# Collected words in four loads on ScalarE's queue, their tables on SyncE's, cleared by VectorE, and a third buffer for the turned adjacency

## The chip, the cores and the metric

The kernel runs on one core of a Trainium2 chip. A time is the device time of one execution in microseconds, the median of several executions. A profiled execution gives a trace besides, from which the stretches and waits below are read. The engines are called PE (TensorE), PEld (its weight loads), DVE (VectorE), ACT (ScalarE), POOL (GpSimd) and SP (SyncE). SP and ACT issue nearly all DMA transfers here, each in its own program order.

## What is computed

A stack of four graph layers on 16 graphs of 1024 nodes with 64 channels, each layer added to its input after a layer norm and a relu. Nearly all of what is difficult lies in the first layer, which drops some edges and then takes, for every node and channel, a weighted sum of three quantiles over the node's neighbours:

```python
rem = neigh & (sk > 1) & (rank % sk == sk - 1) & mask[:, :, None]
rem = rem | jnp.swapaxes(rem, 1, 2)
nd = jnp.where(rem, 0.0, adj_) > 0
s = jnp.sort(jnp.where(nd[..., None], x[:, None, :, :], jnp.inf), axis=2)
nv = nd.sum(2)
for tau, w in zip((0.25, 0.5, 0.75), (0.25, 0.5, 0.25)):
    pos = tau * (nv - 1)
    lo, hi = floor(pos), ceil(pos)
    agg = agg + w * (s[lo] + (pos - lo) * (s[hi] - s[lo]))
y = relu((x + agg) @ W1 + b1) @ W2 + b2
```

The second layer is a gated unit over relu(A m), the third a small network over x and A h, the fourth a graph attention with a softmax over 0.8 A + 0.2 e. All three use the whole adjacency A, so each graph's 4 MB adjacency is needed both as it is and turned.

## The kernel before

The 16 graphs are handled in eight pairs. For every pair there are five kinds of work.

- `sort_pair` and `sort_begin` sort each channel's values over the nodes (DVE, with loads and stores through DRAM on SP's queue).
- `neighbours` reads the adjacency row block by row block (`a`, L819, SP), makes the neighbour bits (L820 DVE, L821 POOL) and their running count (L825 DVE), and turns each 128 x 512 piece on PE (L831). ACT copies the turned piece from PSUM into a tile `at` (L832, two buffers, L833) and stores it to DRAM as `a_d` (L834, ACT's queue). A further stage on ACT and DVE marks the dropped edges, and PE writes their transposes (L875).
- `weights` and `select` find the quantiles. The kept-edge matrix times one-hot codes of the sorted values gives packed counts, "words", by matmul (L1040); ACT and DVE compare them (L1050, L1098, L1114), and PE picks the values by a table `vtab` (L1143), filled by 24 small loads on SP's queue (L930). A node whose words do not suffice is collected: `compact`, at the end of `select`, computes the missing words of up to 64 collected nodes of a batch (L1231), ACT copies them to `xr` (L1237), and SP stores them to DRAM as `x_d` in four pieces (the pieces are those of `PIECES`, two groups of 512 columns each, the last of one).
- `extras` does for the collected nodes of both batches what `select` did for the others: it loads their words (`comb_x`, L1250, one transfer of 1792 KB on SP's queue), clears two tables `tab0`, `tab1` (L1254, POOL) and fills each by four small loads (L1256, ACT's queue), computes `qx` (L1262, DVE), and for three quantiles compares the words (`y_x` L1268 ACT, transposes L1275 PE, `sign_x` L1278 ACT, maxima DVE). PE picks the values (`cand`, L1299, from `tab` and `sign_x`), DVE sums them (L1006, L1013, L1015), PE spreads the sums to their nodes with `sel_t` (L1307, L1310), and a predicated copy writes them into the aggregate.
- `layers` runs the four layers, loading the turned adjacency `adjT` from `a_d` (SP).

The pairs overlap by hand-written program order: `layers` of a pair is written first, then `neighbours` and `sort_pair` of the next pair and `sort_begin` of the one after it. The Tile framework's scheduler merges these into one fixed order per engine when the kernel is compiled; at run time each engine goes through its list in order and waits on semaphores where an operand or a buffer isn't ready. An engine's DMA issues stand in the same list as its other instructions. The work of later pairs thus fills `extras` and `layers`, and starts already at the end of `select`. The last pair has nothing to be filled with, and the first is preceded by about 437 us in which the first sort and the first `neighbours` run alone.

Tiles of `extras` are in a pool `xs`, those of `neighbours` in a pool `nb` that is open beside `xs` and `layers`.

Of the kernel before, what the change touches and what calls it, by code (L numbers as in the profile page):

```python
# [9 lines left out]
F32 = mybir.dt.float32  # L10
# [13 lines left out]
P = 128  # L24
# [18 lines left out]
def gnn_stack(ctx, tc, x, adj, nodemask, w, out):  # L43
# [10 lines left out]
    nc = tc.nc  # L54
# [101 lines left out]
    x_d = dram.tile([P, NW * C], F32, name="x_d")  # L156
# [648 lines left out]
    def neighbours(b, ndT, row10, qb, qz, nb, nbp):  # L805
# [9 lines left out]
        for t0 in range(0, NT, HT):  # L815
            cum = nb.tile([P, HT, N], F16, name="cum")
            for t in range(t0, t0 + HT):
                a = nb.tile([P, N], F32, name="a", bufs=2)
                nc.sync.dma_start(a, adj[b, t * P : (t + 1) * P, :])  # L819
                nc.vector.tensor_single_scalar(ni[:, t, :], a, 0.0, op=ALU.is_gt, saturate=False)  # L820
                nc.gpsimd.tensor_mul(  # L821
                    ni[:, t, t * P : (t + 1) * P], ni[:, t, t * P : (t + 1) * P], offdiag, saturate=False
                )

                nc.vector.tensor_tensor_scan(  # L825
                    cum[:, t - t0, :], ni[:, t, :], wide[:, t, pad - 1 : pad - 1 + N], 0.0, op0=ALU.add, op1=ALU.add
                )
                for q in range(0, NT, 4):
                    pt = nbp.tile([P, 4, P], F32, name="pk")
                    for k in range(4):  # L830
                        nc.tensor.transpose(pt[:, k, :], a[:, (q + k) * P : (q + k + 1) * P], ident)  # L831
                    at = nb.tile([P, 4, P], F32, name="at", bufs=2)  # L832
                    nc.scalar.copy(at, pt)  # L833
                    nc.scalar.dma_start(  # L834
                        a_d[b % 4, q : q + 4, :, t * P : (t + 1) * P].rearrange("j p n -> p j n"), at
                    )


            sk = nb.tile([P, 4, HT], F32, name="sk")
            nc.vector.tensor_tensor(sk[:, 2, :], cum[:, :, N - 1], ni[:, t0 : t0 + HT, N - 1], op=ALU.add)  # L840
            nbi = nb.tile([P, HT], I32, name="nbi")
            nc.vector.tensor_scalar_add(nbi, sk[:, 2, :], 2.0)
            nc.vector.tensor_single_scalar(nbi, nbi, 2, op=ALU.logical_shift_right)
            nc.vector.tensor_single_scalar(sk[:, 0, :], sk[:, 2, :], 2 * MAX_DEGREE, op=ALU.is_gt)
            nc.vector.tensor_mul(sk[:, 0, :], sk[:, 0, :], mask[:, t0 : t0 + HT])
            nc.vector.tensor_copy(sk[:, 1, :], nbi)
            nc.vector.scalar_tensor_tensor(sk[:, 1, :], sk[:, 1, :], 1.0, sk[:, 0, :], op0=ALU.add, op1=ALU.mult)
            nc.vector.tensor_scalar(sk[:, 2, :], sk[:, 1, :], -3.0, 4.0, op0=ALU.mult, op1=ALU.add)
            nc.vector.tensor_scalar_add(sk[:, 1, :], sk[:, 1, :], -1.0)
            nc.vector.scalar_tensor_tensor(sk[:, 3, :], sk[:, 1, :], -1.0, sk[:, 1, :], op0=ALU.mult, op1=ALU.mult)  # L850
            for t in range(t0, t0 + HT):
                k = t - t0
                sq = nb.tile([P, N], F32, name="sq")
                nc.scalar.activation(sq, cum[:, k, :], AF.Square, bias=sk[:, 2, k : k + 1], scale=1.0)  # L854
                nc.scalar.activation(sq, sq, AF.Square, bias=sk[:, 3, k : k + 1], scale=1.0)
                nc.scalar.activation(rem[:, t, :], sq, AF.Relu, bias=one, scale=-1.0, saturate=False)  # L856


                for blocks, to in (
                    ([(j, t) for j in range(t + 1)], ndT[:, : t + 1, t * P : (t + 1) * P]),  # L860
                    ([(t, i) for i in range(t)], ndT[:, t, : t * P].rearrange("p (i n) -> p i n", n=P)),
                ):
                    for n, (j, i) in enumerate(blocks):
                        if n % 4 == 0:
                            pk = nbp.tile([P, 4, P], F32, name="pk")
                        terms = [
                            (ni[:, i, j * P : (j + 1) * P], ident_b),
                            (rem[:, i, j * P : (j + 1) * P], minus_b),
                            (minus_b, rem[:, j, i * P : (i + 1) * P]),
                        ]  # L870
                        if i == j:
                            terms.append((ident_b, ident_b))
                        last = n % 4 == 3 or n == len(blocks) - 1
                        for m, (lhs, rhs) in enumerate(terms):
                            nc.tensor.matmul(  # L875
                                pk[:, n % 4, :], lhs, rhs, start=(n % 4 == 0 and m == 0),
                                stop=(m == len(terms) - 1 and last),
                            )
                        if last:
                            n0, m = n - n % 4, n % 4 + 1  # L880
                            nc.scalar.activation(to[:, n0 : n + 1, :], pk[:, :m, :], AF.Relu, saturate=False)
# [22 lines left out]
        nc.vector.tensor_sub(coef[:, :, :, 0], shares, coef[:, :, :, 1])  # L904


    def weights(b, sb):

        node = sb.tile([P, NT, 4, C], F16, name="node")
        nc.sync.dma_start(node[:, :, 0, :], y_d[b])
        positive = sb.tile([P, NT, C], BF16, name="positive", bufs=2)
        nc.sync.dma_start(positive, p_d[b])
        for k in range(1, 4):
            nc.vector.tensor_scalar_add(node[:, :, k, :], node[:, :, 0, :], 4.0 * CODE * k)
        wt = {}
        for g in PIECES:
            wt[g] = sb.tile([P, NT, 8, C], F8, name="wt", bufs=len(PIECES) + 2)
            for k in range(0, 8, 4):  # L920
                nc.vector.tensor_scalar(  # L921
                    wt[g][:, :, k : k + 4, :].bitcast(U8), node, 4.0 * (25 + CODE * (8 * g + k)), 4.0 * 26,
                    op0=ALU.add, op1=ALU.min,
                )
        rows = w_d[b * C : (b + 1) * C]
        for part, d_, w0, n in ((0, 4, 0, 32), (1, 4, 40, 32), (2, 16, 32, 8)):
            src = rows.rearrange("(q d) w e -> d w q e", d=d_)
            to = vtab[:, part].rearrange("p (q d e) -> p q d e", d=d_, e=24)
            for d in range(d_):
                nc.sync.dma_start(to[d : d_ * n : d_, :, d, :], src[d, w0 : w0 + n])  # L930
        return wt, positive


# [312 lines left out]
    def extras(pr, kept, aggs, xs, xp):  # L1246

        vx = kept["vx"]
        comb = xs.tile([P, NW * C], F32, name="comb_x")
        nc.sync.dma_start(comb, x_d)  # L1250
        tabs = []
        for i in range(2):
            tab = xs.tile([4 * NH, NQ, 4, 48], F16, name=f"tab{i}")
            nc.gpsimd.memset(tab, 0.0)  # L1254
            for d in range(4):
                nc.scalar.dma_start(  # L1256
                    tab[d : 4 * NH : 4, :, d, :],
                    t_d[(pr * 2 + i) * C : (pr * 2 + i + 1) * C, :NH].rearrange("(q d) h e -> d h q e", d=4)[d],
                )
            tabs.append(tab)  # L1260
# [44 lines left out]
        for i in range(2):  # L1305
            sel_t = xs.tile([P, NT, P], F32, name="sel_t")
            nc.sync.dma_start(sel_t, sel_d[i])  # L1307
            ps = xp.tile([P, 2, 512], F32, name="tr")[:, 0, :].rearrange("p (t c) -> p t c", c=C)
            for t in range(NT):
                nc.tensor.matmul(ps[:, t, :], sel_t[:, t, :], aggx, start=True, stop=True)  # L1310
            nc.vector.copy_predicated(
                aggs[i], kept["flag"][i].rearrange("p (t o) -> p t o", o=1).to_broadcast([P, NT, C]), ps
            )


    def layers(b, side_, agg, ly, lb):
# [235 lines left out]
    with nb_ as nb, nbp_ as nbp:  # L1552
        sort_pair(0, sort_begin(0, nbp), nbp)
        made = prepare(0, nb, nbp)
        if pairs > 1:
            cur = sort_begin(1, nbp)
    for pr in range(pairs):
        with tc.tile_pool(reuse_waits="tile", name="keep", bufs=1) as keep:
            aggs = [keep.tile([P, NT, C], F32, name=f"agg{i}") for i in range(2)]
# [4 lines left out]
            with tc.tile_pool(reuse_waits="tile", name="kn", bufs=1) as kn:  # L1564
                with (
# [4 lines left out]
                    tc.tile_pool(reuse_waits="tile", name="sc", bufs=2, space=PSUM) as sc,  # L1570
                ):
                    for i in range(2):
                        wt, positive = weights(pr * 2 + i, kn)
                        select(pr * 2 + i, i, wt, positive, *made[i], aggs[i], kept, sw, sg, sy, sc, sp)
            nb_, nbp_ = side_pools()
            with nb_ as nb, nbp_ as nbp:
                with tc.tile_pool(reuse_waits="tile", name="xs", bufs=1) as xs, tc.tile_pool(reuse_waits="tile", name="xp", bufs=1, space=PSUM) as xp:
                    extras(pr, kept, aggs, xs, xp)
                with (
                    tc.tile_pool(reuse_waits="tile", name="ly0", bufs=1) as ly0,  # L1580
                    tc.tile_pool(reuse_waits="tile", name="ly1", bufs=1) as ly1,
# [57 lines left out]
```

## Time and profile before

| quantity | value |
| --- | --- |
| median of 3 runs | 6583.64 us (6575.58 to 6585.77) |
| the profiled execution | 6593.77 us |
| its span, first to last instruction | 6592.0 us |
| mean granted TensorE clock | 0.821 |
| one pair, from y_x to the next pair's y_x, first seven pairs | 771 to 781 us |
| DMA engines' mean rate | 86 GB/s |

A pair's stretch between the last copy of collected words (L1237) and the first `y_x` (L1268) is called its front below. The first `y_x` of the eight pairs starts at 926.6, 1700.6, 2481.1, 3252.2, 4029.7, 4806.2, 5580.0 and 6315.0 us. From there to the end of `extras` are 94 to 100 us in the first seven pairs and 78 us in the last, and then 189 to 195 us of `layers` in every pair.

How to read the lines that follow: a group line gives line, engine, operation, out<-in with the size, and count; then busy us, mean ns of one; then the idle time of its engine just before it and what ended most of that. The chain is followed back from the last instruction, at each step to what released it.

### The profile page before, as it was taken

How to read it: one execution, taken by the hardware profiler on the slowest of the kernel's cores; microseconds unless marked ns; L12 is line 12 of the kernel's file. 1: busy time of each engine (PE TensorE's matmuls, PEld its weight loads, DVE VectorE, ACT ScalarE, POOL GpSimd, SP SyncE). 2: the span in 40 equal slices, each digit the busy share in tenths (PEclk: the TensorE clock that was granted, in tenths of full speed). 3: DMA queues.
4: the chain of work that ended last, by engine and by line, in shares of the span. 5: the costliest groups of instructions: out<-in, count | busy, mean ns of one | idle time of the engine just before them, and what ended most of it. 6: DMA issues, size and time to landing. Idle time of an engine off the chain costs nothing.

```text
span 6592.0 us, 112930 instructions
## 1 busy us (share of the span) xinstructions
PE 4547.7 (69%) x45010; PEld 2830.8 (43%) x45010; DVE 5323.9 (81%) x13015; ACT 3548.0 (54%) x4348; POOL 180.7 (3%) x250
## 2 busy tenths in 40 slices
PE   0167858777577776778587785777757876778856
PEld 0144544355434444355443554344543544435532
DVE  7759985999769996799949997599967999576645
ACT  0165646556456556565555565556555664555623
POOL 0000000000000000000000000000010000000000
PEclk9868868888688887889788886888868887788967
DMA  1320136211451124401262114511145013520024
GB/s 56 111 70 32 58 99 186 65 44 46 131 177 40 49 87 143 128 33 58 84 189 75 38 52 118 181 52 50 61 146 150 32 56 91 168 76 16 7 61 133
DMA packets 522184, 568.15 MB, mean 86 GB/s; under 512 B 264620, under 2 KB 414510, under 8 KB 520622
## 3 DMA queue, kind: packets, MB, share of 16 engines
q1 hardware_dynamic: 353056, 488.35, 24.3%
q10 hardware_dynamic: 167822, 70.38, 3.8%
q8 instruction: 355, 5.82, 0.4%
q0 software_dynamic: 768, 2.10, 0.1%
q14 instruction: 183, 1.50, 0.1%
HBM read 376.95 MB, written 183.76 MB: 85 GB/s over the span
## 4 chain that ended last, share of the span: by engine, by line
PE 45%; DVE 22%; ACT 17%; DMA 12%; issue 4%; ACTq 0%; SPq 0%; POOL 0%; DVEq 0%; POOLq 0%
PE comb L1040 18%; PE cand L1143 6%; ACT sign L1098 6%; PE comb L1096 5%; PE bank L1401 4%; DMA adjT<-a_d 4%; DMA a_d<-at 3%; ACT y L1050 2%; PE comb L1231 2%; DVE y L1114 2%; DVE cum L825 2%; DVE att L1511 2%; PE pk L875 1%; DVE adjT L1505 1%; DMA a<-in_adj_dram 1%
## 5 line engine op out<-in xcount | busy, mean ns | idle before, releaser
L1040 PE MATMUL comb<-wt,ndT 128*128 128x512 fp8e5 x6144 | 1496.2, 400 | 26.1 <-DVE wt L921 9.0
L1050 ACT ACTIVATE y<-comb,qb 128x1024 int16<-128x1024 f32 (+1 forms) x640 | 630.6, 1026 | 957.0 <-PE comb L1040 956.5
L1040 PEld LDWEIGHTS <-ndT 128*128 128x128 fp8e5 x6144 | 612.9, 103 | 763.2 <-issue 155.3
L1114 DVE TENSOR_TENSOR y<-y 128x512 uint16<-128x512 uint16 (+5 forms) x896 | 702.9, 789 | 65.7 <-PE comb L1096 51.7
L1143 PE MATMUL cand<-vtab,sign 128*128 128x48 f16 (+1 forms) x18432 | 685.2, 193 | 63.4 <-ACT sign L1098 29.2
L1143 PEld LDWEIGHTS <-sign 128*128 128x128 fp8e5 x18432 | 653.8, 97 | 135.0 <-issue 34.6
L1096 PE MATMUL comb<-ident_b,y 128*128 128x128 bf16 x4608 | 390.6, 254 | 434.2 <-ACT sign L1098 381.4
L1098 ACT ACTIVATE sign<-comb,half 128x2048 fp8e5<-128x2048 int16 (+1 forms) x384 | 591.6, 1541 | 127.2 <-PE comb L1096 118.4
L1098 ACT ACTIVATE sign<-comb,lower 128x2048 fp8e5<-128x2048 int16 (+1 forms) x384 | 591.0, 1539 | 0.0
L1151 DVE COPY_PREDICATED cand<-w_f,cand 128x256 f32<-128x256 uint16 (+1 forms) x1536 | 528.3, 376 | 68.4 <-PE cand L1143 66.3
L1096 PEld LDWEIGHTS <-y 128*128 128x128 bf16 x4608 | 356.9, 115 | 458.1 <-issue 451.6
L825 DVE TENSOR_TENSOR_SCAN cum<-ni 128x1024 f16<-128x1024 fp8e5 x128 | 292.8, 2294 | 124.1 <-ACT sq L854 107.0
L1401 PE MATMUL bank<-adjT,nd 128*64 128x512 f32 x1024 | 322.1, 685 | 77.8 <-DMA adjT<-a_d 73.1
L1401 PE MATMUL bank<-att,hs 128*64 128x512 f32 x512 | 210.1, 905 | 197.7 <-ACT hs L1516 197.2
L875 PE MATMUL pk<-ident_b,ni 128*128 128x128 bf16 x1024 | 221.8, 242 | 152.9 <-ACT at L833 87.6
L833 ACT COPY at<-pk 128x512 f32<-128x512 f32 x256 | 146.9, 585 | 319.6 <-DMA a_d<-at 241.5
L729 DVE TENSOR_TENSOR swapped<-s 128x512 uint16<-128x512 f32 x440 | 302.0, 686 | 8.8 <-ACT s L717 2.7
L736 DVE TENSOR_TENSOR s<-s 128x512 f32<-128x512 f32 (+2 forms) x440 | 288.3, 655 | 0.0
L737 DVE TENSOR_TENSOR s<-s 128x512 f32<-128x512 f32 (+2 forms) x440 | 288.2, 655 | 0.0
L921 DVE TENSOR_SCALAR wt<-node 128x2048 uint8<-128x2048 f16 x224 | 265.6, 1219 | 21.8 <-PE comb L1231 21.7
L875 PE MATMUL pk<-minus_b,rem 128*128 128x128 bf16 x1024 | 225.8, 247 | 77.8 <-ACT rem L856 77.8
L760 DVE TENSOR_TENSOR code<-code,xo 128x1024 uint16<-128x1024 uint16 x360 | 265.7, 738 | 5.1
(300 smaller groups left out, 8132.6 us busy)
## 6 DMA issues: line engine op xcount, KB each, us to landing
adjT<-a_d SPq DMA_DIRECT2D x384, 512.0 KB
a<-in_adj_dram SPq DMA_DIRECT2D x128, 512.0 KB
a_d<-at ACTq DMA_DIRECT2D x256, 256.0 KB
m_d<-swapped SPq DMA_DIRECT2D x104, 512.0 KB
swapped<-m_d SPq DMA_DIRECT2D x104, 512.0 KB
n_d<-nat SPq DMA_DIRECT2D x128, 128.0 KB
comb_x<-x_d SPq DMA_DIRECT2D x8, 1792.0 KB
x_d<-xr SPq DMA_DIRECT2D x48, 256.0 KB
```

Source lines behind the costliest of these rows:

```text
L729: nc.vector.tensor_tensor(side(swapped[:, k, :], j), hi, lo, op=ALU.is_gt)
L736: nc.vector.tensor_tensor(to_lo, lo, hi, op=ALU.max)
L825: nc.vector.tensor_tensor_scan(cum[:, t - t0, :], ni[:, t, :], wide[:, t, pad - 1 : pad - 1 + N], 0.0, op0=ALU.add, op1=ALU.add)
L875: nc.tensor.matmul(pk[:, n % 4, :], lhs, rhs, start=(n % 4 == 0 and m == 0), stop=(m == len(terms) - 1 and last),)
L1040: nc.tensor.matmul(pw[:, e, :], ndT[:, j, t * P : (t + 1) * P], piece[:, j].rearrange("p w c -> p (w c)"), start=(j == 0), stop=(j == NT - 1),
L1050: nc.scalar.activation(y[:, 0, chunks, at : at + words_ * d_].rearrange("p q (w d) -> p q w d", d=d_), by_word[:, : words_ * C].rearrange( ...
L1096: nc.tensor.transpose(pt[:, q - q0, :], y[:, 0, q, :].bitcast(BF16), ident_b)
L1098: nc.scalar.activation(signs[tl][s][:, q0:q1, :], pt.bitcast(I16), AF.Sign, bias=before[s], scale=-1.0, saturate=False,)
L1114: nc.vector.tensor_tensor(v[:, :, :, :n], v[:, :, :, :n], v[:, :, :, n : 2 * n], op=ALU.max)
L1143: nc.tensor.matmul(cand[:, e, at : at + 12 * d_].rearrange("p (d l) -> p d l", l=12), signs[tl][sec][:, chunk, :], tab[:, q, :, half_ * 12 ...
L1151: nc.vector.copy_predicated(v[:, :, :, dst : dst + k], mk.to_broadcast([P, 2, C // 2, k]), v[:, :, :, frm : frm + k])
L1401: nc.tensor.matmul(po[to : to + C, :], lhs, rhs[:, f * HALF : (f + 1) * HALF], start=(j == 0), stop=(j == NT - 1))
```

## The change

Five edits. The `comb_x` load becomes four loads by the pieces of `x_d` (three of 512 KB, one of 256 KB), issued on ACT's queue instead of SP's. The tables are cleared by DVE instead of POOL. Their eight loads a pair are issued on SP's queue instead of ACT's. `extras` returns the last of these loads, and `weights` of the next pair's first batch tells the scheduler to put the first of its `vtab` loads, and those after it, behind that load in SP's order of issue. The turned adjacency `at` has three buffers instead of two, 2 KB more in each partition.

```diff
@@ neighbours
-                    at = nb.tile([P, 4, P], F32, name="at", bufs=2)
+                    at = nb.tile([P, 4, P], F32, name="at", bufs=3)
@@ weights
-    def weights(b, sb):
+    def weights(b, sb, behind):
...
+        order = ExitStack()
         rows = w_d[b * C : (b + 1) * C]
         for part, d_, w0, n in ((0, 4, 0, 32), (1, 4, 40, 32), (2, 16, 32, 8)):
             src = rows.rearrange("(q d) w e -> d w q e", d=d_)
             to = vtab[:, part].rearrange("p (q d e) -> p q d e", d=d_, e=24)
             for d in range(d_):
+                if behind is not None:
+                    order.enter_context(tc.issue_after(behind))
+                    behind = None
                 nc.sync.dma_start(to[d : d_ * n : d_, :, d, :], src[d, w0 : w0 + n])
+        order.close()
         return wt, positive
@@ extras
         comb = xs.tile([P, NW * C], F32, name="comb_x")
-        nc.sync.dma_start(comb, x_d)
+        for u in range(0, len(PIECES), 2):
+            at = slice(PIECES[u] * 512, (PIECES[u] + len(PIECES[u : u + 2])) * 512)
+            nc.scalar.dma_start(comb[:, at], x_d[:, at])
         tabs = []
         for i in range(2):
             tab = xs.tile([4 * NH, NQ, 4, 48], F16, name=f"tab{i}")
-            nc.gpsimd.memset(tab, 0.0)
+            nc.vector.memset(tab, 0.0)
             for d in range(4):
-                nc.scalar.dma_start(
+                taken = nc.sync.dma_start(
                     tab[d : 4 * NH : 4, :, d, :],
                     t_d[(pr * 2 + i) * C : (pr * 2 + i + 1) * C, :NH].rearrange("(q d) h e -> d h q e", d=4)[d],
                 )
...
+        return taken.ins if hasattr(taken, "ins") else taken
@@ the loop over pairs
+    taken = None
     for pr in range(pairs):
...
-                        wt, positive = weights(pr * 2 + i, kn)
+                        wt, positive = weights(pr * 2 + i, kn, None if i else taken)
...
-                    extras(pr, kept, aggs, xs, xp)
+                    taken = extras(pr, kept, aggs, xs, xp)
```

## The prediction

> **What bounds the kernel now.** I read the page first (parts 1 and 4), then the stretch in which the edited lines stand. The page names no single engine as the bound:
>
> ```profile
> PE 4547.7 (69%) x45010; PEld 2830.8 (43%) x45010; DVE 5323.9 (81%) x13015; ACT 3548.0 (54%) x4348; POOL 180.7 (3%) x250
> PE 45%; DVE 22%; ACT 17%; DMA 12%; issue 4%; ACTq 0%; SPq 0%; POOL 0%; DVEq 0%; POOLq 0%
> L833 ACT COPY at<-pk 128x512 f32<-128x512 f32 x256 | 146.9, 585 | 319.6 <-DMA a_d<-at 241.5
> ```
>
> DVE is busiest, yet only 22% of the chain that ended last is DVE: latencies in turn set the time, so a stall can be worth its full length where nothing fills it. The copy of the turned adjacency (L833) costs 146.9 us and stands 241.5 us more waiting until an earlier store has freed one of its two buffers.
>
> Second, the tile that the change moves off ACT and POOL:
>
> ```profile
> L1256 ACTq DMA_DIRECT2D tab<-t_d x64: 782/785/5817, 918.8 to 6314.1; - x64
> L1254 POOL MEMSET tab<- x16: 2657/2657/2802, 904.8 to 6290.3; 112x3072 f16 x16
>   ACT y_x L1268: 74.5, 5
> ```
>
> Third, ACT's timeline at the start of extras of the third pair, typical of the middle ones (columns: start, us, what, idle before it and what ended that):
>
> ```profile
> 2447.72 0.58 ACT L1237 COPY xr<-comb 64x512 f32<-64x512 f32 x1 [1.65 <-DMA x_d<-xr]
> 2463.00 0.59 ACT L833 COPY at<-pk 128x512 f32<-128x512 f32 x1 [2.16 <-DMA a_d<-at]
> 2466.23 0.59 ACT L833 COPY at<-pk 128x512 f32<-128x512 f32 x1 [2.65 <-DMA a_d<-at]
> 2467.31 13.70 ACTq L1256 DMA_DIRECT2D tab<-t_d  x8
> 2481.06 6.46 ACT L1268 ACTIVATE y_x<-comb_x,qx 128x3584 int16<-128x3584 f32 x2 [14.24 <-DMA vtab<-w_d]
> ```
>
> The last collected words are copied at 2448.3, and the first use of them (y_x) begins at 2481.06: 33 us in which ACT does eight L833 copies with their waits (to 2466.9) and then stands in eight table issues. SP's timeline has the load of comb_x issued at 2463.56, and its queue events land it at 2474.47, 10.9 us later: y_x could have begun 6.6 us sooner. The chain of this stretch shows why the eight issues took 13.7 us and not 8 x 0.785 = 6.3: the first waited for POOL's two clears, later ones for other loads, down to a vtab load of SP's.
>
> ```profile
> 2462.74 4.57 POOL tab L1254 x2
> 2467.31 10.57 DMA tab<-t_d
> 2477.90 0.59 SPq L930
> 2478.53 2.54 DMA vtab<-w_d
> ```
>
> Fourth, the windows table (columns: busy us of PE, PEld, DVE, ACT, POOL, then clock, DMA share, GB/s) for this front, the rest of extras and the layers, and the last pair's front:
>
> ```profile
> 2448.00:2481.00 33.00, 10.08 (x172) 8.53 (x170) 31.95 (x73) 4.89 (x9) 8.81 (x9) 0.75 0.87 251
> 2481.00:2579.00 98.00, 58.34 (x799) 49.40 (x799) 68.64 (x149) 66.10 (x71) 3.06 (x7) 0.65 0.33 95
> 2579.00:2768.00 189.00, 139.62 (x722) 63.69 (x723) 129.63 (x350) 106.31 (x153) 7.69 (x10) 0.83 0.57 171
> 6302.00:6315.00 13.00, 4.89 (x144) 4.67 (x144) 7.08 (x27) 0.03 (x1) 0.00 (x0) 0.85 0.77 235
> ```
>
> In the front DVE is full, but with fill (neighbours and sorting of later pairs); the DMA engines are 0.87 busy. The front is 31.6 to 33.4 us long in the first seven pairs and 13 in the last, which has no next pair beside it.
>
> **What the Trainium skill says.** "DMA: Bandwidth & Descriptors", section "Issuing engines are not separate DMA queues": transfers started by different engines run on the same 16 DMA engines, and spreading them saves only the issuing sequencer's time. The trace agrees: ACT loses 0.785 us for each table issue while its loads share an 0.87 busy front. So moving the comb_x load to ACT makes it no faster; only issuing it sooner could. Same page, "Anatomy of one DMA — SWDGE (gpsimd) path": DMA engines wait on no semaphore, the issuing sequencer does. The trace agrees for these queues: y_x stood behind issues that waited. "VectorE: DVE Perf Modes", section "Zero memsets can be issued as uint32 (trn2)": a clear costs a cycle an element, and a 2-byte one can go at half the elements. The trace has this for vtab (L142: 2304 uint32 in 1.978 us, 0.859 ns each), so a table of 3072 f16, 1536 words, is 1.32 us.
>
> **Part by part.** Sums are against the profiled execution, 6593.77 us (span 6592.0); the median of the runs, 6583.64, is 10.1 lower, and I take savings from that.
>
> *Tables off ACT's queue.* ACT loses eight issues a pair. y_x then waits for comb_x alone. On ACT the four pieces of that load follow the eight L833 copies, because the program order that the compiler keeps puts extras' first instructions beside the end of the values (DVE's qx at 2466.39, right behind the last sum), not where x_d has landed (2452.6 by the queue's events). With three buffers the eight copies end some 4 us earlier: first piece at about 2462.5, four issues of 0.8, landing 10.9 us after the first as the single load did, since bytes and traffic are the same: 2473.4. y_x gains 2481.0 - 2473.4 = 7.6 us. Seven pairs: 53. In the last pair, comb_x is issued at 6304.64 and lands at 6313.29, with y_x at 6314.97; the two DVE clears now precede qx (6311.2 + 2.6 = 6313.8): gain 1.2. From both sides: nothing, if pieces land later on the busy engines, and 20 us a pair, if they go out once x_d is there (2452.6 + 8.65 = 2461.3, the landing of a quiet load).
>
> *Clears on DVE.* 16 x 1.32 = 21 us on DVE (42 if not halved), POOL's 42.5 us gone; POOL was 3% busy. In the front DVE is full, but displaces fill that can be done in the windows behind it (68.6 of 98 and 129.6 of 189 us busy). I charge a third of seven pairs' 2.64: 6 us. Without that cover it is 18.
>
> *Tables on SP.* Eight issues of 0.785, 6.3 us a pair, on a queue that also issues adjacency and sorting loads. They can start when the clears end (about 2469), and must have landed by the first L1299, 8.4 us after y_x (2489.42 against 2481.06), at about 2482; quiet, a load lands in 2.5 us, so about 2478 to 2480. Tight but covered; uncovered, it costs up to the front's gain (7.6).
>
> *vtab loads behind the tables.* An order, no wait. 24 issues at 0.6 us, 14.5 us, as now (17 of them take 10.57 from 2480.81); they are first needed by the next pair's values, some 350 us later. Nothing; if they move ahead of adjacency loads, a few us.
>
> *Third buffer for L833.* Its waits on a store are 10.6 to 17.2 us in the fronts (counted above), by windows of the third pair 9.4 in the rest of extras and 7.1 in the layers; over seven pairs 10.5 and 7 on average. One more buffer lets a copy wait for the third store back; I take half of 17.5 away, 8.7, and half of that as on the path, since the chain has this store in some pairs' windows (12.3% of the 98 us of the third pair) and nearly nowhere in others: 4.4 x 7 = 31. Bounds: 0, if the stores' landing at the same rate is the limit, and 12 a pair.
>
> Sum: 53 + 1 + 31 - 6 = 79. Profiled 6593.8 - 79 = 6515; as a median 6583.6 - 79 = 6505.
>
> **Rivals.** *Large gain.* The pieces leave as each part of x_d lands and the buffer waits go: 20 x 7 + 12 x 7 = 224, giving 6360. For it: the last pair has a front of 13 us. Against: the queue order above, and the full DMA engines.
>
> *Gain given back.* The front shortens, but what was done in it (copies, sums, sorting) must be done in the windows behind, where the next wait is late instead; DVE's 81% speaks for it. Same here: a compiled order in which the pieces leave no sooner. Only 0 to 20 us remain: 6575.
>
> *Slower: SP's queue stands.* SP issues in order. The table loads wait for DVE's clears, which wait behind a full DVE. Also, a table issue of before began at 6313.31, just when comb_x had landed at 6313.29: issues wait for earlier transfers, and four pieces in flight hold more of them than one did. While SP stands, adjacency and sorting loads and sel_t stand behind it, and PE stands at its first L1299 with the transposes behind it. Price: the front's 53 lost, and 12 us a pair of late loads: 84 - (31 - 6) = 59 slower, 6643. It decides from where the delay exceeds (53 + 25) / 7 = 11 us a pair, counted from y_x + 8.4. For it: on ACT these eight issues took 13.7 us rather than 6.3, and SP may fare the same; against: the times above leave 2 to 4 us to spare, and the fill has other loads in hand.
>
> **How the numbers follow.** Forecast 0.48, own range 6460 to 6550; large gain 0.16; given back 0.13; slower 0.23. A measurement of this kernel tells about 0.2%, 13 us, from no change. Faster: 0.47 + 0.16 + 0.04 = 0.67; same 0.09; slower 0.24. The range of 8 in 10 reaches to half of the large gain and half of the slower case: 6375 to 6640; outside are 0.08 and 0.11.
>
> **What would show it.** Right: no L1256 on ACT; y_x about 25 us after the last xr copy, released by a comb_x load; L833's idle on its store down from 241.5 to about 120; DVE clears near 1.32 us; L1299 without idle on tab. Wrong: y_x at 12 us or at 33; PE idle on DMA tab; SP's a loads late, L820 waiting on them; the L833 wait moved to "PE pk".

## The result, and the profile after

The changed kernel takes 6532.24 us (median of 4 runs, 6518.26 to 6547.95) where the kernel before takes 6579.61 (median of 4 runs taken beside it); the ratio is 0.9924, with a 95% interval of 0.9903 to 0.9944. That is 47 us faster, on the predicted side and about 0.6 of the predicted 79 us. The profiled execution, 6547.95 us, is the longest of the four, some 16 us above their median.

The chain by engine and the copy of the turned adjacency in the page of the changed kernel:

```profile
PE 44%; DVE 23%; ACT 18%; DMA 11%; issue 4%; ACTq 0%; SPq 0%; POOL 0%; DVEq 0%; POOLq 0%
L833 ACT COPY at<-pk 128x512 f32<-128x512 f32 x256 | 146.7, 586 | 334.5 <-DMA a_d<-at 167.6
```

The shares have hardly moved. The copy's waits on its store fell by 74 us (from 241.5), yet all its idle time rose from 319.6 to 334.5. The view of that line's waits in the changed kernel says where it went:

```profile
  DMA a_d<-at: 167.6, 89
  PE pk L831: 132.0, 109
  DMA tab<-t_d: 13.6, 3
  PE cand L1148: 13.5, 3
```

The wait on PE's turned piece was 76.1 us before. Fewer waits of one kind are thus no proof of a gain: most of them were replaced by another. (The copy uses no table. One semaphore serves many transfers in turn, so the transfer named in such a line can be a neighbour of the one that was waited for.)

The tables, in the view of their tile (changed kernel):

```profile
L1263 SPq DMA_DIRECT2D tab<-t_d x64: 772/772/921, 908.4 to 6270.7; - x64
L1261 DVE MEMSET tab<- x16: 1338/1338/1338, 907.1 to 6264.9; 112x1536 uint32 x16
```

The clears are on DVE as uint32, 1.338 us each. ACT's timeline of the third pair's front, as shown for the kernel before:

```profile
2431.11 0.58 ACT L1242 COPY xr<-comb 64x512 f32<-64x512 f32 x1 [2.00 <-DMA x_d<-xr]
2445.83 0.58 ACT L833 COPY at<-pk 128x512 f32<-128x512 f32 x1 [0.52 <-DMA a_d<-at]
2445.85 4.84 ACTq L1257 DMA_DIRECT2D comb_x<-x_d  x4
2451.24 0.58 ACT L833 COPY at<-pk 128x512 f32<-128x512 f32 x1 [4.82 <-DMA a_d<-at]
2457.50 6.46 ACT L1275 ACTIVATE y_x<-comb_x,qx 128x3584 int16<-128x3584 f32 x2 [5.68 <-DMA a_d<-at]
```

The table issues are gone from ACT. The front is 2457.50 - 2431.69 = 25.8 us where it was 32.8. By the queue events the last of the four pieces landed at 2457.39, 0.11 us before y_x: the words end the wait now, although the line names a store. The four issues took 4.84 us, not 4 x 0.5: the fourth left at 2450.37, just after a store had landed at 2450.29. The copy behind them stood 4.82 us.

To compare whole kernels I cut each profiled span at the same events: the first pair's last xr copy, the fronts, extras (y_x to the last predicated copy into the aggregate, which ends some 12 us before the end that is used ahead of the prediction), and the rest. Sums over eight pairs in us, read from the trace:

| kernel | to the first front | fronts | extras | rest |
| --- | --- | --- | --- | --- |
| before | 895.0 | 239.7 | 672.4 | 4784.8 |
| changed | 892.2 | 190.6 | 685.0 | 4778.3 |

Fronts gave 49 us, extras took 13 back. Each row is one profiled execution, and both of these are longer than their kernel's median, by 10 us before and 16 us changed. The windows table of extras of the third pair, before and then changed, shows what came back (columns as in the prediction: PE, PEld, DVE, ACT, POOL, then clock, DMA share, GB/s):

```profile
2481.10:2567.20 86.10, 50.09 (x691) 43.24 (x692) 59.71 (x131) 61.29 (x63) 1.21 (x4) 0.60 0.26 76
```

```profile
2457.50:2545.00 87.50, 51.19 (x776) 44.97 (x777) 70.19 (x156) 63.57 (x67) 3.33 (x7) 0.69 0.30 76
```

DVE does 10.5 us more in extras. That is sorting and neighbours; in the front DVE does 9 us less. Nearly all of it fits into DVE's idle time: extras got only 1.4 us longer here.

### The profile page after: what moved, and what is told of

Read it like the earlier page. It is cut to its first block, busy times and chain, and to the rows that moved or that the text cites. A ratio compares the mean times of both kernels' runs of the same rounds, so it can differ in the third digit from the quotient of the medians.

```text
span 6546.1 us, 112888 instructions
## 1 busy us (share of the span) xinstructions
PE 4538.7 (69%) x45010; PEld 2819.2 (43%) x45010; DVE 5301.1 (81%) x13031; ACT 3545.5 (54%) x4348; POOL 137.5 (2%) x234
## 4 chain that ended last, share of the span: by engine, by line
PE 44%; DVE 23%; ACT 18%; DMA 11%; issue 4%; ACTq 0%; SPq 0%; POOL 0%; DVEq 0%; POOLq 0%
PE comb L1045 17%; PE cand L1148 6%; ACT sign L1103 6%; DMA adjT<-a_d 4%; PE comb L1101 4%; PE bank L1409 4%; DVE y L1119 3%; ACT y L1055 2%; PE comb L1236 2%; DMA a<-in_adj_dram 2%; PE pk L875 2%; DVE att L1519 2%; DVE adjT L1513 2%; DVE cand L1156 2%; DMA a_d<-at 1%
## 5 line engine op out<-in xcount | busy, mean ns | idle before, releaser
L1045 PE MATMUL comb<-wt,ndT 128*128 128x512 fp8e5 x6144 | 1518.2, 404 | 60.3 <-DVE top L1516 29.3
L833 ACT COPY at<-pk 128x512 f32<-128x512 f32 x256 | 146.7, 586 | 334.5 <-DMA a_d<-at 167.6
L875 PE MATMUL pk<-ident_b,ni 128*128 128x128 bf16 x1024 | 217.8, 239 | 145.5 <-ACT at L833 80.0
L921 DVE TENSOR_SCALAR wt<-node 128x2048 uint8<-128x2048 f16 x224 | 267.6, 1216 | 25.8 <-PE comb L1236 25.7
L875 PE MATMUL pk<-minus_b,rem 128*128 128x128 bf16 x1024 | 219.3, 242 | 88.3 <-ACT rem L856 88.3
```

The lines of the kernel that those rows point to most:

```text
L875: nc.tensor.matmul(pk[:, n % 4, :], lhs, rhs, start=(n % 4 == 0 and m == 0), stop=(m == len(terms) - 1 and last),)
L1045: nc.tensor.matmul(pw[:, e, :], ndT[:, j, t * P : (t + 1) * P], piece[:, j].rearrange("p w c -> p (w c)"), start=(j == 0), stop=(j == NT - 1),
```

## The experiments

Eleven kernels were measured on three occasions, and every ratio is to the kernel before on the same occasion (4 to 6 runs of a kernel, 22 of e1 and of e2). The two sums are in us, from one profiled execution each. Each kernel is scheduled anew when it is compiled, so what an edit costs or brings is always that of the edit together with whatever new order of the engines' lists comes with it.

| kernel | ratio (95%) | fronts | extras |
| --- | --- | --- | --- |
| the change | 0.9924 (0.9903 to 0.9944) | 190.6 | 685.0 |
| e1: third buffer alone | 0.9993 (0.9984 to 1.0002) | 224.6 | 669.5 |
| e7: tables on SP alone | 0.9945 (0.9925 to 0.9966) | 196.0 | 677.2 |
| e8: both of these | 0.9882 (0.9866 to 0.9899) | 180.1 | 671.0 |
| e13: both, and the order | 0.9869 (0.9851 to 0.9888) | 171.2 | 676.1 |
| e10: both, clears on DVE | 0.9916 (0.9899 to 0.9933) | 180.5 | 693.8 |
| e11: both, words in four on ACT | 0.9923 (0.9906 to 0.9939) | 193.0 | 675.2 |
| e2: change, two buffers | 0.9983 (0.9975 to 0.9992) | 201.8 | 692.1 |
| e3: change, clears on POOL | 0.9916 (0.9896 to 0.9935) | 182.8 | 683.1 |
| e6: change, words in one on SP | 0.9913 (0.9897 to 0.9929) | 175.1 | 692.8 |
| e5: change, words in one on ACT | 0.9929 (0.9914 to 0.9944) | 190.8 | 686.0 |
| e4: change, no order | 0.9947 (0.9933 to 0.9962) | 200.7 | 686.5 |

**First: one edit alone, or one taken out.**

e1, on the kernel before:

```diff
-                    at = nb.tile([P, 4, P], F32, name="at", bufs=2)
+                    at = nb.tile([P, 4, P], F32, name="at", bufs=3)
```

> Only the third buffer of the turned adjacency, nothing else. Theory 1 (the buffer's waits outside the front are off the path, the gain of the change is all in the front): the tables' issues on ACT still wait for POOL's two clears, which follow the end of the values, so the front stays at 32 us and the time within 10 us of before, ratio 0.9985 to 1.001; the copy's idle on its store falls from 241 to about 170 us while its idle on PE grows by about as much. Theory 2 (the sum's term was right and something else ate it): 25 to 35 us faster, ratio near 0.995.

6578.28 against 6583.47 us: theory 1's number, and no gain that can be told. Its group line:

```profile
L833 ACT COPY at<-pk 128x512 f32<-128x512 f32 x256 | 146.0, 586 | 246.2 <-DMA a_d<-at 136.5 <-PE pk L831 90.9 <-PE cand L1143 10.6
```

105 us of waits on the store are gone and the time stays. The fronts are 2 us a pair shorter (not unchanged, as I had expected); in these two profiles 9 us of that come back in the rest, and the medians leave 5 us of gain.

e2, on the changed kernel:

```diff
-                    at = nb.tile([P, 4, P], F32, name="at", bufs=3)
+                    at = nb.tile([P, 4, P], F32, name="at", bufs=2)
```

> The changed kernel with two buffers for the turned adjacency again. Theory 1: the copies end some 4 us later in the front, the four pieces go out later with them, the front is 26 to 30 us instead of 25.5, and the time is 0 to 28 us above the changed kernel, all of it in the front; ratio to before 0.993 to 0.997. If the pieces' issue isn't held up by the copies at all, the same as the changed kernel (0.9924). Theory 2: 31 us lost, in extras and layers, with the front as in the changed kernel.

6573.09 us, only 0.17% faster than before, and about 38 us (0.59%) slower than the change. That is more than theory 1 allowed, and not in the places that theory 2 named: of the 25 us between the two profiles, 11 us are in the fronts, 7 in extras and 6 elsewhere. Both theories fell: the buffer is worth nothing alone and much in company.

```profile
L833 ACT COPY at<-pk 128x512 f32<-128x512 f32 x256 | 146.9, 586 | 363.6 <-DMA a_d<-at 307.8 <-PE pk L831 47.4 <-DMA comb_x<-x_d 7.0
```

With two buffers in the shortened schedule the copy waits 307.8 us on its store, more than the 241.5 of before. The chain within extras of the fifth pair (the view's line of shares, as far as it is printed; first e2, then the change) shows this wait on the path, twice as long in e2:

```profile
by line: DMA a_d<-at 21.0%; PE pk L875 12.8%; ACT sign_x L1285 12.5%; ACT y_x L1275 9.4%; ACT rem L856 7.5%; ACT sq L854 7.4%; ACT sq L855 7.0%; DMA tab<-t_d 6.9%; PE cand L1306 5.2%; ACT ndT L881 4.9%; ACT at L833 3.5%; issue 3.2%; PE tr L
```

```profile
by line: ACT sign_x L1285 10.8%; PE pk L875 10.6%; DMA a_d<-at 10.5%; ACT rem L856 8.9%; PE cand L1306 7.6%; ACT y_x L1275 7.5%; ACT sq L855 7.3%; ACT sq L854 6.5%; PE pk L831 6.0%; ACT ndT L881 6.0%; DMA a<-in_adj_dram 5.4%; issue 4.8%; PE
```

e7, on the kernel before:

```diff
-                nc.scalar.dma_start(
+                nc.sync.dma_start(
                     tab[d : 4 * NH : 4, :, d, :],
```

> Only the eight table loads go to SP's queue; the clears stay on POOL and the words come in one transfer on SP. Theory 1 (the removed issues on ACT are the whole gain, and the words' own move is worth nothing): y_x waits for the one transfer, which lands 6.5 us before y_x of before: front 25 to 27 us, ratio 0.992 to 0.994. Theory 3 (the words must be issued sooner or in pieces to gain): front 29 to 32 us, ratio 0.997 to 1.0. If SP's order puts table loads ahead of the words' load, the front grows beyond 33 us.

6552.68 us. The fronts of the first seven pairs are 25.2 to 27.2 us, as theory 1 said, with the words in their one transfer on SP. The ratio falls a little short of it, 0.9945. So the removed issues alone shorten the front, by 6 us a pair, and the move of the words isn't needed for it.

e3, on the changed kernel:

```diff
-            nc.vector.memset(tab, 0.0)
+            nc.gpsimd.memset(tab, 0.0)
```

> The changed kernel with the clears on POOL. Theory 1 (the 21 us of clears on DVE are hidden behind fill): within 8 us of the changed kernel, ratio 0.991 to 0.994; the last pair's y_x no longer waits for qx behind the clears and starts 1 to 2 us sooner; the table loads leave about 4 us later, and the first picking matmuls may wait for them by a few us. Theory 4 (the clears cost what DVE spends): 15 to 21 us faster than the changed kernel, ratio near 0.990, with extras shorter by 2 us a pair.

6528.49 us, within the changed kernel's noise. The last pair's front fell from 12.6 to 9.4 us: qx no longer stands behind two clears. Here the clears on DVE look nearly free; e10 will say otherwise.

**Second: which company does the buffer need?** e8 takes e7 and adds the third buffer, nothing else.

> The kernel before with two edits only: tables' loads on SP's queue and three buffers for the turned adjacency. Theory 5 (the third buffer, worth nothing alone, pays 30 us or more as soon as the tables' issues are off ACT, because the copies pushed out of the front into extras wait there on the path): ratio to before 0.988 to 0.9915, so that the words' move to ACT, the clears on DVE and the order of vtab add nothing; extras' chain loses half of its 21% of waits on the store. Theory 6 (the third buffer pays only for the four pieces on ACT's queue, which hold up the copies): as with the tables alone, 0.9935 to 0.9955.

6508.33 us, 76 below before and, by the ratios, some 28 below the whole change. Theory 5 is right in its number: the buffer pays 0.63% on top of the tables (0.9945 to 0.9882), and nothing alone. Its fronts lose 16 us against e7 and its extras 6; 18 more lie in the rest. The fronts' part can be followed: the words' load leaves 14.3 us after the last xr copy instead of 15.9, and y_x begins 0.1 us after it has landed instead of 1.2 (means of seven pairs). In the third pair's extras its copies wait:

```profile
  PE pk L831: 8.2, 6
  DMA a_d<-at: 5.7, 4
```

The expected halving of the store's wait on the chain can't be read, since e8's chain is followed back only to about 5.8 ms. The copies' own waits on their store in extras are nearly halved (third pair 10.7 us in e7, 5.7 here; all pairs 71.6 and 39.1), but most of that turns up as longer waits on PE (26.3 and 51.5). Nor were copies "pushed out of the front": it has 8 of them in before, e7 and e8 alike. What changed is the order behind it, with 8, 10 and 11 copies in extras.

The 18 us in the rest have a rival that these runs don't exclude. All runs of e8 were granted 0.829 to 0.831 of TensorE's clock, those of e7 0.822 to 0.826, those of the kernel before 0.818 to 0.826. In the rest PE is busy 3648 us in e7 and 3626 in e8. So nearly half of the buffer's gain here may be a faster PE and not a wait that went away. Whether the schedule brings the higher clock isn't shown. A profile of e13 below, 20 us above its own kernel's median, has a rest 22 us longer than e8's, so one profile's rest proves little.

The other three are the changed kernel with one edit taken out. e6 and e5 replace the four loads:

```diff
-        for u in range(0, len(PIECES), 2):
-            at = slice(PIECES[u] * 512, (PIECES[u] + len(PIECES[u : u + 2])) * 512)
-            nc.scalar.dma_start(comb[:, at], x_d[:, at])
+        nc.sync.dma_start(comb, x_d)
```

(e5 has `nc.scalar` in the last line).

> The changed kernel with the words in one transfer on SP again. Theory 5: within 8 us of the changed kernel, ratio 0.991 to 0.9935, front 25 to 27 us. Theory 6 or any worth of the move itself: 15 to 40 us slower than the changed kernel, ratio 0.9945 to 0.998, with a longer front.

> The changed kernel with the words in one transfer on ACT's queue, not in four. Theory 5: y_x needs all four pieces, so that splitting brings nothing: within 8 us of the changed kernel, ratio 0.991 to 0.9935. If four issues, each of which may wait for an earlier transfer (in the changed kernel they took 4.84 us of ACT in the third pair), hold up the copies, one load is faster by up to 2 us a pair, ratio near 0.990.

6528.57 and 6537.23 us, both indistinguishable from the change. Splitting brings nothing, and costs nothing either: in the third pair e5's one issue holds ACT for 0.63 us where the change's four hold it for 4.84, and yet the fronts are equally long (190.8 and 190.6 us). In e6 the fronts are 15.5 us shorter than in the change and extras 7.8 longer: moving the words to ACT lengthens the front, and here half of that is given back behind it. From the first issue to the last landing the words take 11.5 us in the change, 11.6 in e5 and 9.8 in e6 (means of seven pairs, by the queue events).

e4, on the changed kernel:

```diff
-                        wt, positive = weights(pr * 2 + i, kn, None if i else taken)
+                        wt, positive = weights(pr * 2 + i, kn, None)
```

> The changed kernel without the order between the tables' loads and the next pair's vtab loads. Theory 5: the order costs and brings nothing, ratio 0.991 to 0.9935. If it matters, some vtab loads go out ahead of the tables again, as in the kernel before, the tables land later by 2 us a pair, and the time is up to 15 us longer (0.994).

6552.33 us, ratio 0.9947: at the expected upper end of a loss, 0.23% above the change, though the intervals overlap. The fronts are 10 us longer.

**Third: the price of the parts that e8 leaves out.** Each adds one of them to e8: the clears on DVE, the four loads on ACT, the order.

> The kernel of the two edits (tables on SP, third buffer) with the clears on DVE. Theory 7 (the clears, 2.64 us a pair in front of qx and of the table loads, cost what DVE spends on them): 10 to 21 us slower than the two edits, ratio to before 0.990 to 0.9915, last pair's front longer by 1 to 3 us. Theory 1 (hidden behind fill): within 6 us of the two edits, 0.9875 to 0.989.

6535.25 us, 22 us (0.34%) more than e8 by the ratios, which were taken on two occasions and whose intervals just touch: theory 7's size. The loss isn't where I had looked, in front of qx. Fronts are the same (180.5 against 180.1), and extras are 22.8 us longer. From the second to the sixth of the collected sums (L1015) DVE spends, besides 10.5 us on them, 3.0 us of fill in each of pairs 3 to 6, 2.5 of it sorting; in e8 less than 1. That stretch takes 23.1 to 24.2 us where e8 takes 20.6 to 21.3. Lines of DVE's timeline between two such sums (others left out), first e10, then e8:

```profile
4054.76 0.28 DVE L1015 SCALAR_TENSOR_TENSOR agg_x<-cand,vx,agg_x 128x64 f32<-128x64 f32 x1
4055.03 0.41 DVE L754 TENSOR_TENSOR xo<-xo,swapped 128x512 uint16<-128x512 uint16 x1
4057.60 0.42 DVE L757 TENSOR_TENSOR code<-code,xo 128x512 uint16<-128x512 uint16 x1
4059.32 0.96 DVE L1006 COPY_PREDICATED cand<-odd_x,cand 128x768 f32<-128x768 uint16 x1 [1.30 <-PE cand L1299]
4061.84 0.28 DVE L1015 SCALAR_TENSOR_TENSOR agg_x<-cand,vx,agg_x 128x64 f32<-128x64 f32 x1
```

```profile
4032.98 0.28 DVE L1015 SCALAR_TENSOR_TENSOR agg_x<-cand,vx,agg_x 128x64 f32<-128x64 f32 x1
4033.98 0.16 DVE L850 SCALAR_TENSOR_TENSOR sk<-sk 128x4 f32<-128x4 f32 x1
4038.64 0.28 DVE L1015 SCALAR_TENSOR_TENSOR agg_x<-cand,vx,agg_x 128x64 f32<-128x64 f32 x1
```

7.1 us against 5.7. But DVE isn't what is late in e10: it has done its fill by 4058.0 and stands 1.30 us for the picked values. ACT's and PE's timelines of e10, and PE's of e8, name what held the picking matmuls:

```profile
4055.68 0.59 ACT L833 COPY at<-pk 128x512 f32<-128x512 f32 x1 [3.76 <-DMA a_d<-at]
4056.31 0.27 PE L875 MATMUL pk<-ident_b,ni 128*128 128x128 bf16 x1 [4.13 <-ACT at L833]
4056.51 2.77 PE L1299 MATMUL cand<-tab,sign_x 112*64 112x96 f16 x64
```

```profile
4033.32 2.77 PE L1299 MATMUL cand<-tab,sign_x 112*64 112x96 f16 x64 [2.40 <-DVE agg_x L1015]
```

In e10 PE stands 4.13 us at a fill matmul (L875) that is ahead of the picking in its order. That one waits for ACT's copy, and the copy for its store. The picking begins 1.5 us after the sum; in e8 it follows the sum directly. DVE stands for the picked values at this place in six of e10's seven pairs (0.4 to 1.3 us), and in all seven in the interval behind it. There too the picking begins late, 1.0 to 1.3 us after the sum instead of 0.1 to 0.3. So with the clears on DVE the kernel has another order, in which fill comes ahead of the picking on PE. In these two intervals some 2.0 of the 3.3 us a pair come out, and not through DVE's own time. Where the remaining 1.3 us arise I didn't trace.

> The kernel of the two edits with the words in four transfers on ACT's queue, clears still on POOL. Theory 8 (four issues on ACT, each of which can wait for an earlier transfer, hold up the copies and so extras): 10 to 25 us slower than the two edits, ratio 0.990 to 0.992, extras longer by 1 to 3 us a pair. Theory 1 (a move without effect): 0.9875 to 0.989.

6541.46 us, 27 us (0.41%) more than e8: theory 8's size, but not its place. The fronts are 13 us longer, extras 4 us in all instead of 8 to 24, and 21 of the 36 us between the two profiles lie in the rest, where PE is busy 24 us longer. e11's order leaves 8 or 9 copies to extras in most pairs where e8 has 11, and the clock it was granted was lower (0.824 to 0.829), so these 21 us can't be laid to the words' queue. ACT's timeline in the third pair's front of e11:

```profile
2444.46 5.45 ACTq L1252 DMA_DIRECT2D comb_x<-x_d  x4
2452.95 0.59 ACT L833 COPY at<-pk 128x512 f32<-128x512 f32 x1 [7.93 <-DMA comb_x<-x_d]
2457.32 3.28 ACT L1270 ACTIVATE y_x<-comb_x,qx 128x3584 int16<-128x3584 f32 x1 [3.78 <-DMA a_d<-at]
```

By the queue events the third piece left at 2448.95, when a store of 2442.92 had landed at 2448.93; the last piece landed at 2457.22, 12.8 us after the first issue. In e8 the one transfer left SP at 2436.76, 14.5 us after the last xr copy (in e11 the first piece: 14.8), and landed 10.1 us later. On ACT it isn't issued sooner, and the later pieces wait for earlier transfers. Over seven pairs the first issue comes 14.4 us after the last xr copy in e11 and 14.3 in e8, and the last landing 11.7 and 9.6 us after that. These 2.1 us a pair are the longer front. As e5 shows the same with a single issue, the pieces' waits for each other aren't the reason; why the words take longer in ACT's queue stays open.

> The kernel of the two edits with the order of the vtab loads behind the tables. If the order helps here as it did in the changed kernel (14 us): ratio 0.986 to 0.987 with table loads done sooner. If it only counts where the words go out on ACT: 0.9875 to 0.989. If the order keeps sorting or adjacency loads waiting: above 0.990.

6504.96 us, ratio 0.9869: not told from e8 (0.9882). The order does no harm, and may help by a few us. This is the lowest time found, with the two edits of e8 doing the work: both beat the kernel before and the whole change.

**All eight combinations.** With tables on SP and three buffers, every combination of the other three edits has now been measured (ratio, then fronts and extras together in us):

| words | clears | without the order | with the order |
| --- | --- | --- | --- |
| one load on SP | POOL | e8: 0.9882, 851 | e13: 0.9869, 847 |
| one load on SP | DVE | e10: 0.9916, 874 | e6: 0.9913, 868 |
| four loads on ACT | POOL | e11: 0.9923, 868 | e3: 0.9916, 866 |
| four loads on ACT | DVE | e4: 0.9947, 887 | the change: 0.9924, 876 |

Averaged over the four pairs that differ in one edit alone, the clears on DVE cost 18 us, the words on ACT 21, and the order brings 8. Each of these is uncertain by some 8 us (an estimate from the ratios' intervals, taken as independent).

## Why the prediction came out as it did

- **The front.** Predicted 7.6 us a pair, 53 in seven pairs, and 1.2 in the last. The changed kernel's seven fronts sum to 178.0 us instead of 226.7: 48.7, or 7.0 a pair; the last gave 0.4. The steps held too: the first piece left 14.2 us after the last xr copy, which is what the prediction's 2462.5 - 2448.3 says, and the pieces landed 11.5 us after that, where it had 10.9. Its reason was right as well: e7 has the short front without moving the words. The buffer's share in the front was put at some 4 us a pair: with two buffers (e2) the first piece leaves 3.1 us later than in the change, but the pieces then land 1.6 us faster.
- **Third buffer.** The prediction put 31 us for it outside the front, as a term of its own. Alone it is worth 0.07%, which can't be told from nothing (e1); with the tables off ACT 0.63% (e8 against e7); in the changed kernel 0.59% (e2). A sum of separate terms can't say this. In the new orders more copies stand in extras (8 in the third pair before and in e1, 10 in e7 and e2, 11 in the changed kernel and e8), where the store's wait can end on the path, as e2's chain shows. But of what e8 gains over e7, only 6 us are in extras and 16 are in the fronts; the rest is open. So "half of that as on the path" came near in size, and where the gain lies it didn't say.
- **The sum of these two.** 53 + 1 + 31 is 85; e8 measured 76. That is near in part by luck: in e8's profile the fronts gave 60 us instead of 54, extras 1, and the rest 20, where waits on the store can't be told from a faster PE.
- **The step that failed** is the cost of the other parts. The clears were charged "a third of seven pairs' 2.64: 6 us", hidden in windows with idle DVE. The prediction's bound "Without that cover it is 18" was the better value: on the two edits alone they cost 22 us (e10), and 18 on the average of four comparisons. But the bound's reason was DVE's time, and e10's trace has most of the loss on PE, in the new order. The words' move was counted at no cost ("makes it no faster"); on the two edits it cost 27 us (e11), and 21 on the average. The part of it that the traces show in every comparison is the front, 12 to 20 us longer. The prediction let the pieces land 10.9 us after the first issue "as the single load did, since bytes and traffic are the same"; on seven pairs' average they took 11.5, where the one load took 9.5 before. Without both edits e13 is 0.55% below the change, some 36 us, and that is the missing part of the sum. Taken out of the whole change one at a time (e3, e6) they gain nothing that can be told; whether the two prices add is not settled by these intervals.
- **The order.** Counted at nothing. e4 points to some 15 us in the changed kernel, with overlapping intervals, and e13 to 9. In the traces the fronts are shorter with it in all four pairs of the table (by 5 to 10 us), and in two of them extras take a part back. It probably brings a little.
- **Rivals.** The slower case didn't come about: the table loads took 11.5 us of SP from 2448.49 and the last landed at 2461.77, 4.1 us ahead of the first picking matmul at 2465.86, and that line shows no idle time on a table in the changed kernel. "Gain given back" held in part, as extras rose by 13 us in all, but not for its reason: e8's third-pair extras hold as much of DVE's work (69.2 us, 70.2 in the change, 59.7 before) and are shorter than before (85.3 us against 86.1). The large gain was excluded as argued: the words left 13.9 us after the last xr copy in the change and 14.3 in e8, where that rival needed about 4 (before 16.0).
- **The shown sign "L833's idle on its store down to about 120"** was a poor one. It went to 167.6, in e1 to 136.5 without any gain.

## What to carry to other kernels

Take DMA issues off an engine whose next instruction is on the critical chain, and look at what the issue itself waits for: here eight 0.8 us issues held ACT 13.7 us. A wait that is hidden today can be on the path once its neighbour goes, so test edits in pairs as well as alone; here one buffer was worth 0 or 40 us. And an operation is not free because its engine is idle in the windows behind: where each engine's order is fixed at compile time, an edit can give all engines a new order, and the loss can come out on another engine, so look where the work comes out.

## What the runs showed of the hardware

Eight table issues of 0.772 us each took 11.5 us on SP in the changed kernel and 13.30 in e8, as they had taken 13.7 on ACT: on either queue they wait for earlier transfers to land. The eight completion semaphores of this program are used in turn by the transfers of both queues, and five of the changed kernel's eight table issues in the third pair began 0.01 to 0.07 us after the landing of the transfer that had the same semaphore before. Moved to SP, these waits no longer stood ahead of y_x.

With three buffers, the 1792 KB of words landed 9.2 to 9.8 us after their issue on SP (means of e6, e8, e10, e13) and 11.4 to 11.7 us after the first issue on ACT, in one piece or four (the change, e3, e4, e5, e11). With two buffers on ACT (e2) it was 9.9. The cause is open.

DVE's clear of 112 x 3072 f16 ran as 1536 uint32 in 1.338 us, half of POOL's 2.657.
